# A gate that takes raw rows: centred weights, and 1 / std applied to the gate's result

## The chip, the cores and the metric

The kernel runs on one core of a Trainium2 chip. The metric is device time in microseconds, the median of several executions. The engines are TensorE (PE, its weight loads shown apart as PEld), VectorE (DVE), ScalarE (ACT), GpSimd (POOL) and SyncE (SP), which issues most DMAs. Each engine works through its own queue in order, and waits there for what an instruction needs from others.

## The reference

8192 tokens (2 sequences of 4096) of 512 channels:

```python
xn = _layernorm(x, axis=-1)                # (x - m) / sqrt(v + eps), no affine part
s = recurrence(xn, delta, alpha, beta, gamma, omega)   # causal convolution per channel, plus xn * omega
gate_logits = xn @ Wg.T + bg               # 8 experts
topk_vals, topk_idx = top_k(gate_logits, 2)
gate_w = softmax(topk_vals)
ffn = sum over the two experts of gate_w * (xn @ We[e].T + be[e])
out = x + s * silu(ffn)
```

All of it is float32.

## The kernel before

The work has three stages on one core, and their order on every engine is the order of the program: a helper (`InOrder`, lines 31 to 58) chains each instruction to the one before it on its engine, and all of them are recorded at its line 58.

Setup and first stage (lines 446 to 714). Tokens come in 64 chunks of 128, four chunks (`LC`) to a group, 16 groups (`NQ`). `load(q)` brings group q, 1 MB, into one of four buffers `xt_b` (`NX`). The recurrence's kernel is made first: VectorE, GpSimd and ScalarE make exponentials, GpSimd `coef_w`, and TensorE adds 256 small matmul instructions up in the PSUM tile `k_ps` (lines 547 to 557). `kernel_out` takes `k_ps` through VectorE and stores it to `k_dram`.

Then a loop over q runs these helpers:
- `stats_of(q)`: VectorE's mean and variance of four chunks, into `stats[:, c, 2:4]`. `stats_of(0)` stands right after the `k_ps` matmuls in the program.
- `root(q)`, on ScalarE, and `rest(q)`, on VectorE: `stats` then holds -mean / std and 1 / std.
- `apply(q, i, engine)`: one chunk is normalised from `xt_b` into `xn`, which lies in `big` as (channel, chunk), so that one chunk's channels lie 64 elements apart. Chunk 0 of a group is ScalarE's, the others are GpSimd's, a few VectorE's.
- `turn_chunk(q - 1, i)`: TensorE transposes four blocks of the chunk into a PSUM tile `pt`, and ScalarE copies that back into `xt_b`, over the rows of x.
- `gate(q - 1)`: 16 f32 matmuls (32 instructions) with `wg_sb` as the loaded weights and the transposed rows moving, into `lq`; VectorE copies it to `lqs`.
- `gate_end(q - 2)`: TensorE turns `lqs` back into `lt`; VectorE adds the bias and writes `logits`.
- `load(q + 3)`, on SyncE's queue, once `gate(q - 1)` has read the buffer.

Line 636 on is the loop itself, with its order. The `pt`, `lq`, `lt` tiles share six PSUM buffers (`ps_y`). After the loop the last group is transposed (line 697), the recurrence is begun (`states`, `scan`, `from_chunks`), and the last two groups' gates are done between (lines 709 to 714).

Second stage (lines 967 to 998): the recurrence over 64 groups of channels. Between its groups stand the routing steps, at group 2 `top2(0)`, which reads all logits. `double_toep` copies a group's matrix to the other half of the partitions, on ScalarE for even groups, on GpSimd for odd ones. Third stage (line 1003 on): two passes of experts over sorted tokens, with indirect gathers and scatters by GpSimd.

Of the kernel before, what the change touches and what calls it, by code (L numbers as in the profile page):

```python
# [8 lines left out]
FP = mybir.dt.float32  # L9
# [4 lines left out]
ALU = mybir.AluOpType  # L14
AX = mybir.AxisListType

P = 128
# [44 lines left out]
def tile_ssm_then_moe(  # L62
# [28 lines left out]
    C, _, D = x_rev.shape  # L91
    T = C * P
    NE = w_e.shape[0]
    KD = D // P
# [22 lines left out]
    ident = const.tile([P, P], FP)  # L117
# [4 lines left out]
    io = InOrder(tc)  # L122
# [9 lines left out]
    def bc(ap, *shape):  # L132
        return ap.to_broadcast(list(shape))
# [160 lines left out]
    with ExitStack() as ab:  # L294
        abc = ab.enter_context(tc.tile_pool(name="ab_const", bufs=1))

        xn = big[:, 0:4, :].rearrange("p i (d c) -> p (i d) c", c=C)
# [10 lines left out]
        stats = abc.tile([P, C, 4], FP)  # L308
        gate_b = abc.tile([P, NE], FP)
        flip = abc.tile([P, P], FP)  # L310
        logits = abc.tile([P, C, NE], FP)
# [8 lines left out]
        ps_y = ab.enter_context(tc.tile_pool(name="ps_y", bufs=NR + 2, space=PSUM))  # L320
# [26 lines left out]
        def double_toep(g):  # L347

            copy = io.scalar.copy if g % NS in TO_ACT else io.gpsimd.tensor_copy
            copy(toep_of(g, 1 - g % 2), toep_of(g, g % 2))  # L350
# [95 lines left out]
        with ExitStack() as ph0:  # L446
            su = ph0.enter_context(tc.tile_pool(name="setup", bufs=1))
            xtp = ph0.enter_context(tc.tile_pool(name="xnT", bufs=2))

            LC = 4  # L450
            NQ = C // LC
            NX = 4

            xt_b = [
                big[:, 4, i * LC * D : (i + 1) * LC * D].rearrange("p (c d) -> p c d", d=D)
                for i in range(NX)
            ]

            def load(q):
                io.sync.dma_start(  # L460
                    out=xt_b[q % NX], in_=x_rev[q * LC : (q + 1) * LC].rearrange("c p d -> p c d")
                )
# [3 lines left out]
            wg_sb = su.tile([P, KD, 32], FP)  # L466
            io.sync.dma_start(out=par, in_=params)
            load(0)
            io.gpsimd.memset(wg_sb, 0.0)
            io.sync.dma_start(out=om, in_=omega)  # L470
            io.sync.dma_start(out=wg_sb[:, :, 0:NE], in_=w_g)
            io.sync.dma_start(out=gate_b, in_=b_g.to_broadcast([P, NE]))
# [25 lines left out]
            q = su.tile([P, G], FP)  # L498
# [6 lines left out]
            def stats_of(q):  # L505
                st = xtp.tile([P, LC, 6], FP, tag="st")
                for i in range(LC):
                    io.vector.bn_stats(st[:, i, :], xt_b[q % NX][:, i, :])
                    io.vector.bn_aggr(stats[:, q * LC + i, 2:4], st[:, i, :])
# [38 lines left out]
            for n, (tl, bq) in enumerate(units):  # L548
                for a in range(2):
                    for i in range(IL):  # L550
                        for j in range(NR):
                            g = (tl * NR + j) * NB + 2 * bq + a
                            io.tensor.matmul(
                                k_ps[32 * j : 32 * j + 32, tl, i, :], coef_w[:, g, i, :],
                                ex_b[:, n, j, a, :], start=n == 0 and a == 0 and i == 0,
                                stop=n == len(units) - 1 and a == 1 and i == IL - 1,
                            )
            stats_of(0)
            io.scalar.activation(q_half, lnq, AF.Exp, scale=float(H))
            powers = {}  # L560
# [44 lines left out]
            def turn_chunk(q, i):  # L605
                pt = ps_y.tile([P, KD, P], FP, tag="py", name="pt")
                for k in range(KD):
                    io.tensor.transpose(
                        pt[:, k, :], xn[:, k * P : (k + 1) * P, q * LC + i], ident
                    )  # L610
                io.scalar.copy(xt_b[q % NX][:, i, :], pt.rearrange("p k t -> p (k t)"))

# [14 lines left out]
            def gate_end(q):  # L627
                lt = ps_y.tile([P, LC, 32], FP, tag="py", name="lt")
                io.tensor.transpose(lt.rearrange("p c j -> p (c j)"), lqs_of.pop(q), ident)
                io.vector.tensor_add(  # L630
                    logits[:, q * LC : (q + 1) * LC, :], lt[:, :, 0:NE],
                    bc(gate_b.unsqueeze(1), P, LC, NE),
                )

            toeps = {}
# [2 lines left out]
            for q in range(NQ):  # L638
# [7 lines left out]
                if q >= 1:  # L646
                    for i in range(LC):
                        turn_chunk(q - 1, i)
                if q >= 2:
                    gate_end(q - 2)  # L650
# [45 lines left out]
            for i in range(LC):  # L696
                turn_chunk(NQ - 1, i)
# [9 lines left out]
            toeps[TB - 1] = load_toep(TB - 1)  # L707
            double_toep(DOUBLED)
            gate_end(NQ - 2)
            gate(NQ - 1)  # L710
            from_chunks(0, 1, pys0, toeps.pop(1))
            toeps[TB] = load_toep(TB)
            double_toep(DOUBLED + 1)
            gate_end(NQ - 1)


        rt = ab.enter_context(tc.tile_pool(name="route", bufs=1))
# [407 lines left out]
```

## Time and profile before

| | us |
|---|---|
| median of 3 runs (lowest, highest) | 931.26 (927.09, 931.91) |
| profiled execution: time | 937.24 |
| profiled execution: span, first to last instruction | 935.5 |
| TensorE busy over the span (7035 matmul instructions) | 813.0 |
| VectorE busy | 608.4 |
| ScalarE busy | 379.2 |
| GpSimd busy | 511.9 |
| granted TensorE clock, mean | 0.942 |

The first stage takes about the first 98 us, the recurrence goes on to about 312 us, and the experts take the rest. Busy times are those of one profiled execution. A row of a timeline has the start and the length in us, the engine, the line, the operation, what it writes and reads, how often it came in that stretch, and in brackets the idle time of the engine ahead of it with what ended it.

### The profile page before, as it was taken

How to read it: one execution, taken by the hardware profiler on the slowest of the kernel's cores; microseconds unless marked ns; L12 is line 12 of the kernel's file. 1: busy time of each engine (PE TensorE's matmuls, PEld its weight loads, DVE VectorE, ACT ScalarE, POOL GpSimd, SP SyncE). 2: the span in 40 equal slices, each digit the busy share in tenths (PEclk: the TensorE clock that was granted, in tenths of full speed). 3: DMA queues.
4: the chain of work that ended last, by engine and by line, in shares of the span. 5: the costliest groups of instructions: out<-in, count | busy, mean ns of one | idle time of the engine just before them, and what ended most of it. 6: DMA issues, size and time to landing. Idle time of an engine off the chain costs nothing.

```text
span 935.5 us, 18673 instructions
## 1 busy us (share of the span) xinstructions
PE 813.0 (87%) x7035; PEld 479.3 (51%) x7038; DVE 608.4 (65%) x1147; ACT 379.2 (41%) x699; POOL 511.9 (55%) x513
## 2 busy tenths in 40 slices
PE   3989878886885799999999999995989797899876
PEld 3767657776765454444444444442434343444432
DVE  7877676768783656666666663264768575576675
ACT  7777646766762322222222121232434333244242
POOL 6767204431444355555555556576767675767732
PEclk9999968998997799999999999998999898989978
DMA  4656115768899875555555566577676766866740
GB/s 157 224 212 183 25 30 28 179 143 212 230 220 336 241 261 203 182 187 190 202 201 183 203 206 237 185 261 245 202 241 207 243 206 199 251 197 214 251 146 28
DMA packets 112822, 181.22 MB, mean 194 GB/s; under 512 B 18910, under 2 KB 68446, under 8 KB 112736
## 3 DMA queue, kind: packets, MB, share of 16 engines
q0 software_dynamic: 38128, 127.05, 40.8%
q1 hardware_dynamic: 74608, 52.99, 21.6%
q8 instruction: 58, 0.95, 0.4%
q14 instruction: 28, 0.23, 0.1%
HBM read 112.50 MB, written 73.01 MB: 198 GB/s over the span
## 4 chain that ended last, share of the span: by engine, by line
PE 39%; issue 16%; DVE 14%; POOL 13%; ACT 8%; DMA 6%; another core or an unknown queue 4%; POOLq 0%; SPq 0%; DVEq 0%; ACTq 0%
PE pe L58 26%; PE pt L58 5%; ACT big L58 5%; DVE big L58 4%; POOL big L58 4%; DVE came_b L58 4%; PE py L58 4%; POOL out L58 3%; DMA toep_b<-k_dram 2%; PE ph L58 2%; DMA big<-yx_dram,x_idx 2%; POOL sg L58 2%; POOL yx_dram L58 1%; POOL yx L58 1%
## 5 line engine op out<-in xcount | busy, mean ns | idle before, releaser
L58 PE MATMUL pe<-big,xnT 128*128 x672 | 311.7, 608 | 0.0
L58 PE MATMUL pe<-big 128*128 x464 | 214.6, 607 | 0.7 <-DMA s_dram<-big 0.7
L58 PEld LDWEIGHTS pe<-big,xnT 128*128 128x128 f32 x672 | 125.0, 196 | 127.2 <-issue 127.2
L58 PEld LDWEIGHTS pe<-big 128*128 128x128 f32 x464 | 86.0, 195 | 89.2 <-issue 88.9
L58 ACT COPY xnT<-pt 128x512 f32<-128x512 f32 x84 | 48.9, 582 | 202.8 <-PE pt L58 123.5
L58 POOL DMA_INDIRECT out<-big,o_idx x71 | 78.6, 1107 | 71.5 <-DVE big L58 53.6
L58 ACT COPY big<-pt 128x512 f32<-128x512 f32 x122 | 68.8, 597 | 116.7 <-PE pt L58 90.4
L58 PEld LDWEIGHTS pt<-ident,big 128*128 128x128 f32 x544 | 75.5, 198 | 69.8 <-issue 38.1
L58 PE MATMUL pt<-ident,big 128*128 128x128 f32 x544 | 87.5, 299 | 27.1 <-ACT xnT L58 13.5
L58 ACT ACTIVATE big<-big 128x512 f32<-128x512 f32 x103 | 65.8, 649 | 110.9 <-DVE big L58 69.9
L58 PE MATMUL py<-big,toep_b 64*64 64x64 f32 x2048 | 89.1, 243 | 15.9 <-issue 6.6
L58 PEld LDWEIGHTS py<-big,toep_b 64*64 64x64 f32 x2048 | 78.2, 153 | 27.3 <-issue 12.3
L58 POOL DMA_INDIRECT yx_dram<-big,o_idx x47 | 47.8, 1017 | 74.2 <-DVE big L58 72.4
L58 POOL TENSOR_TENSOR val<-hot,token 128x568 bf16<-128x568 bf16 x32 | 39.2, 1226 | 81.1 <-DVE hot L58 42.9
L58 PEld LDWEIGHTS pt<-ident,xn 128*128 128x128 f32 x280 | 35.4, 145 | 63.1 <-issue 43.0
L58 POOL TENSOR_SCALAR big<-big,stats 128x512 f32<-128x512 f32 x44 | 55.8, 1348 | 21.1 <-ACT stats L58 11.3
L58 PE MATMUL pt<-ident,xn 128*128 128x128 f32 x280 | 44.1, 282 | 24.7 <-ACT xnT L58 14.9
L58 POOL DMA_INDIRECT big<-in_x,x_idx x52 | 51.4, 988 | 23.0 <-issue 16.0
L58 DVE TENSOR_TENSOR big<-pe,big 128x512 f32<-128x512 f32 x47 | 32.5, 692 | 48.1 <-PE pe L58 38.2
L58 POOL DMA_INDIRECT sg<-s_dram,x_idx x42 | 48.0, 1142 | 13.1 <-issue 11.0
L58 POOL COPY toep_b<-toep_b 64x512 f32<-64x512 f32 x32 | 23.6, 743 | 53.8 <-DMA toep_b<-k_dram 52.4
L58 DVE TENSOR_TENSOR big<-big 128x512 f32<-128x512 f32 x73 | 50.3, 689 | 3.4 <-issue 1.2
(154 smaller groups left out, 1158.4 us busy)
## 6 DMA issues: line engine op xcount, KB each, us to landing
big<-in_x_rev SPq DMA_DIRECT2D x16, 1024.0 KB
s_dram<-big SPq DMA_DIRECT2D x64, 256.0 KB
toep_b<-k_dram SPq DMA_DIRECT2D x64, 128.0 KB
big<-in_w_e SPq DMA_DIRECT2D x16, 512.0 KB
big<-in_b_e SPq DMA_DIRECT2D x8, 256.0 KB
out<-big,o_idx POOLq DMA_INDIRECT x71
big<-in_x,x_idx POOLq DMA_INDIRECT x52
yx_dram<-big,o_idx POOLq DMA_INDIRECT x47
```

Of the source, the lines that this page charges most:

```text
L58: return lambda *args, **kwargs: self.order.follow(make(*args, **kwargs))
```

## The change

The transposes, and with them the gate, take the rows of x as loaded. Layer norm's mean is taken out through the weights: each expert's column of `wg_sb` is centred over the 512 channels once, with a mean from four matmuls by a matrix of 1 / 512 (`mean_w`, filled by GpSimd in the setup) and a subtraction on VectorE ahead of `stats_of(0)`. 1 / std multiplies each group's gate result in `gate_end`, and the bias is added once to all logits, on GpSimd, after the last group.

```diff
             io.gpsimd.memset(wg_sb, 0.0)
+            mean_w = su.tile([P, P], FP)
+            io.gpsimd.memset(mean_w, 1.0 / D)
             io.sync.dma_start(out=om, in_=omega)
...
+            wm = ps_y.tile([P, 32], FP, tag="py", name="wm")
+            for k in range(KD):
+                io.tensor.matmul(wm, mean_w, wg_sb[:, k, :], start=k == 0, stop=k == KD - 1)
+            io.vector.tensor_sub(wg_sb, wg_sb, bc(wm.unsqueeze(1), P, KD, 32))
             stats_of(0)
...
                     io.tensor.transpose(
-                        pt[:, k, :], xn[:, k * P : (k + 1) * P, q * LC + i], ident
+                        pt[:, k, :], xt_b[q % NX][:, i, k * P : (k + 1) * P], ident
                     )
...
-                io.vector.tensor_add(
-                    logits[:, q * LC : (q + 1) * LC, :], lt[:, :, 0:NE],
-                    bc(gate_b.unsqueeze(1), P, LC, NE),
+                cs = slice(q * LC, (q + 1) * LC)
+                io.vector.tensor_tensor(
+                    logits[:, cs, :], lt[:, :, 0:NE],
+                    bc(stats[:, cs, 3].unsqueeze(2), P, LC, NE), ALU.mult,
                 )
...
             gate_end(NQ - 1)
+            io.gpsimd.tensor_tensor(logits, logits, bc(gate_b.unsqueeze(1), P, C, NE), ALU.add)
```

The normalised rows are still made, by the same passes, since the recurrence needs them.

## The prediction

> **What bounds the kernel now.** I read the stage busy times first: up to about 98 us the first stage (norm, transposes, gate) runs, to 312 us the recurrence, then the experts. The change touches the first stage and the gate's end, so I opened the timeline of the first 60 us, all engines together. In it, "big<-big,stats" is a normalising pass, "big<-pt" a copy of transposed rows, and root, rest, gate are the functions of those names.
>
> ```profile
> 10.71 6.49 PE L58 MATMUL k_ps<-big 128*32 128x64 f32 x256 [10.71 <-ACT big L58]
> 11.13 0.68 DVE L58 BATCH_NORM_STATS2 st<-big 128x6 f32<-128x512 f32 x1
> ...
> 14.23 0.18 DVE L58 BATCH_NORM_AGGREGATE stats<-st 128x2 f32<-128x6 f32 x1
> ...
> 16.05 0.30 ACT L58 ACTIVATE stats<-stats,eps 128x4 f32<-128x4 f32 x1
> 16.39 0.18 DVE L58 RECIPROCAL stats<-stats 128x4 f32<-128x4 f32 x1 [1.98 <-ACT stats L58]
> ...
> 17.37 1.53 ACT L58 ACTIVATE big<-big,stats 128x512 f32<-128x512 f32 x1 [1.02 <-DVE st L58]
> ...
> 20.76 0.39 DVE L58 COPY came_b<-k_ps 128x256 f32<-128x256 f32 x1
> ...
> 23.03 2.11 ACT L58 COPY big<-pt 128x512 f32<-128x512 f32 x4
> ```
>
> To be seen: VectorE finishes the statistics of chunk group 0 at 14.41, under the k_ps matmuls that keep TensorE until 17.20. It then idles 1.98 us for ScalarE's square root (16.05), so rest(0) is early at 16.39; from there to 21.65 VectorE runs without a gap (statistics of group 1, one normalise, k_ps out, rest(1)). ScalarE's first copies come at 23.03, behind its second normalise.
>
> In the loop, one of its slower turns:
>
> ```profile
> 26.30 0.29 DVE L58 COPY lqs<-lq 128x128 f32<-128x128 f32 x1 [0.53 <-PE lq L58]
> ...
> 27.30 0.70 DVE L58 BATCH_NORM_STATS2 st<-big 128x6 f32<-128x512 f32 x1 [0.71 <-DMA big<-in_x_rev]
> ...
> 30.64 0.30 ACT L58 ACTIVATE stats<-stats,eps 128x4 f32<-128x4 f32 x1 [1.16 <-DVE stats L58]
> ...
> 31.39 1.54 ACT L58 ACTIVATE big<-big,stats 128x512 f32<-128x512 f32 x1 [0.45 <-DVE stats L58]
> ...
> 32.68 2.13 ACT L58 COPY big<-pt 128x512 f32<-128x512 f32 x4
> ...
> 33.41 2.51 PE L58 MATMUL lq<-big,wg_sb 128*32 128x128 f32 x32 [0.17 <-ACT big L58]
> ```
>
> Gate(0) ends at 26.26, frees lqs and its buffer's next load; statistics (3.3), root and rest (0.75), normalise on ScalarE (1.3), four copies (2.13), last 26 gate matmuls (1.06), and gate(2) ends at 35.92: 9.66 us for two turns. A second circle runs through the four x buffers: a load takes some 5.4 us (issued 21.86, waited for until 27.30), and 5.4 + 8.5 us of the same steps is about 14 for three turns. Fifteen turns from 20.99 to 96.08 make 5.0 us each. TensorE looks full, but its weight loads wait 15.9 us in total for ScalarE's copies, and the transposes are in neither circle, except where the copies keep pace with them (four copies in 2.35 instead of 2.13 us in the faster turns).
>
> **Start: the new wait.** VectorE's subtraction of the column means stands ahead of stats_of(0) in its queue and needs wm, whose matmuls stand behind all 256 k_ps matmuls. Queued behind it: all statistics, root and rest of group 0, group 1, and kernel_out, behind whose k_dram store SyncE's queue holds load(3). wm is four f32 matmuls, each two instructions (the expert groups have eight per four): 8 weight loads of 128x128. Nearest row: contiguous transposes, one per 0.11 us (below), so 0.9 us, and 0.2 to 0.3 for the last to come out; by the 0.19 us duration of an expert's weight load 1.5. From the k_ps end (about 17.0 for the last start): 18.1, at most 18.8. Subtraction, 128x128 with a PSUM operand: lqs copies cost 0.29, so 18.4. Statistics 11.13 to 14.41 are 3.28: 21.7. Root and latency 0.34: rest(0) at 22.1 instead of 16.39. From rest(0) on VectorE had no gap before, so all that follows moves: **+5.7 us** (5.2 with weight loads at half the nearest price, 6.3 with the dear one). The square root's table load is over by 16.05 and not waited for.
>
> **Loop: shorter transposes.** Before, 16 strided transposes; contiguous ones stand in the expert stage, here the weight-load timeline of both:
>
> ```profile
> 26.19 2.42 PEld L58 LDWEIGHTS pt<-ident,big 128*128 128x128 f32 x16 [0.20 <-issue]
> ```
>
> ```profile
> 403.40 0.36 PEld L58 LDWEIGHTS pt<-ident,xn 128*128 128x128 f32 x3 [0.29 <-issue]
> ```
>
> Sixteen starts (to the next load at 28.50) in 2.31 are 0.144 each; three in 0.36, the last lasting 0.14, are 0.11. So some 0.6 us per turn. The Trainium skill, "TensorE: Matmul & The Clock Gate", section LDWEIGHTS, prices a weight load by its columns alone, which would save nothing; the rows differ by stride at equal columns (median 258 against 140 ns), and I take the rows. By the page the tail gain below is zero and the sum 0.65 higher. Within the loop the 0.6 us becomes waiting for copies: those still stand behind ScalarE's normalise, which waits for rest. That the transposes need no normalised rows frees nothing else, since their copies overwrite x and must wait for the normalising passes to have read it. In the loop I take **-0.2**, one load (63.27, which waited 1.16 us) issued earlier; ends 0 and -1.
>
> After the last turn TensorE runs without a gap from the 16 transposes on to the matmuls that release VectorE's scan at 106.74 (the chain of waits):
>
> ```profile
> 96.15 2.55 PE pt L58 x16
> 98.70 1.49 PE ph L58 x64
> ```
>
> Here the saving counts once: **-0.65** (0 to -0.9).
>
> **A cold TensorE at the loop's start.** Freed transposes of group 0 run right behind wm and are done by about 20.2; then TensorE waits until copies(0), 23.03 + 5.7 = 28.7. The windows of 3.41 us in which the clock steps show what such a gap does (columns: length; busy us of PE, PEld, DVE, ACT, POOL; granted clock):
>
> ```profile
> 46.47:49.89 3.42, 2.04 (x15) 1.80 (x13) 2.49 (x8) 3.42 (x8) 2.41 (x3) 1.00 0.81 304
> 49.89:53.30 3.41, 3.07 (x38) 2.07 (x39) 1.11 (x4) 2.96 (x6) 0.75 (x1) 1.00 0.02 5
> ...
> 111.33:114.74 3.41, 1.15 (x22) 0.87 (x22) 3.13 (x7) 3.36 (x7) 0.61 (x1) 0.97 0.17 38
> 114.74:118.15 3.41, 3.28 (x88) 2.77 (x92) 3.27 (x5) 1.59 (x3) 0.00 (x0) 0.50 0.15 38
> ```
>
> A window with 1.15 us of PE halves the clock of the next; the new gap of 8.5 us holds a whole empty one. So gate(0) and transposes(1) start cold. Cold rates: four pw transposes take 1.11 instead of 0.65 us, 32 py matmuls 1.97 instead of 1.18, so 1.7 times. Gate(0)'s last 26: +0.75 us. Transposes(1), 3.0 us instead of 1.8, then pace the copies: gate(1) ends 1.3 to 2 us late. Gate(0)'s 0.75 partly hides under load(3)'s 0.71 us; gate(1)'s delay passes through lqs to the statistics of group 4. I take **+1.2**, ends 0.4 and 3. TensorE is then filled for over 6.8 us, so at least one full window, and warms: the window 128.39 to 131.81, busy throughout, ended a cold stretch. Against that stands the same page, section PE-mode transpose: transposes do not count as busy for the clock. Then the loop stays cold, at some 1.7 us per turn. The first row above speaks against it: that window holds nothing but transposes, and the next is still at 1.00. I take the row; the rule is a rival.
>
> **Rest.** The gate's multiply replaces an add of the same 128x32 shape (0.17 us): nothing. The mean_w memset (0.20 by the wg_sb row) lies in POOL's 0.81 us wait for lnq. The bias add, 128x512 on POOL: 1.34 by the "big<-steps,lnq" row; it waits for the last gate_end (104.76), ends about 106.2, while top2 takes logits at 110.75: hidden by the scan and 4.5 us to spare; without that cover 1.4. POOL's toep copy for group 5 is queued behind it and moves from about 96 to 107; group 5 is multiplied at 122.14. All free.
>
> **Sum:** 5.7 + 1.2 - 0.2 - 0.65 = +6.05. The recurrence and the experts start from the gate's results and the loop's end, and their loads are issued from the same order, so the shift arrives at the end. The profiled execution, 937.24 (935.5 span and what lies around it), becomes 943.3; it was 6.0 above the median of the runs, so the median 931.26 becomes **937.3**.
>
> **Rivals.** (1) The loop is TensorE's after all: 16 x 0.63 = 10.1 us saved, so 5.7 + 1.2 - 10.1 = -3.2, 928.1: not slower. For it: PE is busy over 3.0 of 3.41 us in most windows there. Against: 15.9 us of waits for ScalarE. It decides from 0.46 us reaching the circle per turn (6.9 / 15). (2) The cold loop: 14 x 1.7 = +24, 961. (3) The shift arrives in part: the clock's windows run on their own time, one cold window costs or saves about 1.7 us, and some eight cold stretches lie before 312 us; where two or three fall better, about 933.
>
> **How the numbers follow.** Forecast 0.60, own range 932.5 to 941.5; rival (1) 0.12, (2) 0.08, (3) 0.20. Half a per cent (4.7 us) is about what a measurement tells from no change: 935.9 and 926.6. Slower: 0.85 of the forecast, all of (2), a fifth of (3): 0.63. Faster: a third of (1) and traces of the others: 0.06. Same: 0.31. The range 931 to 946 leaves out most of (1) and all of (2).
>
> **What would show it.** Reciprocal of group 0 near 22 us; a PE gap of 8 us and clock 0.50 there; load(3) issued near 27.5; turns again about 5.0 us; the first scan about 6 us late; POOL's add ending before top2. Wrong if turns shrink to 4.6 us, if the clock stays low beyond about 40 us, or if wm finishes before 17 us.

## The result

Median of 18 runs 935.87 us (927.87 to 944.06), the kernel before beside it 930.17 (923.88 to 939.22): ratio 1.0075, 95% interval 1.005 to 1.010, so 4.7 to 9.3 us slower. The ratio compares fast runs alone and is not the quotient of the two medians, which is 1.0061. The forecast was 937.3 against 931.26, 6.05 us slower.

The changed kernel's timeline from 9 to 62 us, all engines, the rows that answer to those shown of before:

```profile
10.61 6.51 PE L58 MATMUL k_ps<-big 128*32 128x64 f32 x256 [10.61 <-ACT big L58]
17.04 1.08 PE L58 MATMUL wm<-wg_sb,mean_w 128*128 128x32 f32 x8
17.96 1.94 PE L58 MATMUL pt<-ident,big 128*128 128x128 f32 x16
18.16 0.29 DVE L58 TENSOR_TENSOR wg_sb<-wg_sb,wm 128x128 f32<-128x128 f32 x1 [7.06 <-PE wm L58]
...
22.02 0.18 DVE L58 RECIPROCAL stats<-stats 128x4 f32<-128x4 f32 x1 [0.37 <-ACT stats L58]
...
27.30 32.72 SPq L58 DMA_DIRECT2D big<-in_x_rev  x7
...
28.45 2.13 ACT L58 COPY big<-pt 128x512 f32<-128x512 f32 x4
...
29.18 3.37 PE L58 MATMUL lq<-big,wg_sb 128*32 128x128 f32 x32 [9.27 <-ACT big L58]
...
32.58 0.29 DVE L58 COPY lqs<-lq 128x128 f32<-128x128 f32 x1 [1.39 <-PE lq L58]
```

VectorE waits 7.06 us for wm, which TensorE makes behind k_ps. The reciprocal of group 0 comes at 22.02 instead of 16.39, load(3) at 27.30 instead of 21.86, the first copies at 28.45 instead of 23.03, and TensorE stands for 9.27 us ahead of gate(0). From lqs(0), the first copy of a gate's result, to the last group's transposes the loop then takes 69.37 us (32.58 to 101.95), before it took 69.78 (26.30 to 96.08).

The chain of waits behind the loop (start, length, what), first of before, then of the changed kernel:

```profile
106.74 1.28 DVE came_b L58 x2
...
108.11 2.71 DVE came_b L58 x2
```

```profile
102.02 1.90 PE pt L58 x16
103.91 1.49 PE ph L58 x64
...
111.95 1.28 DVE came_b L58 x2
...
113.33 2.34 DVE came_b L58 x2
```

The transposes start 5.87 us later than before (102.02 against 96.15) and VectorE's product behind the ph matmuls 5.21 later. The experts' first product starts 6.49 us later, at 319.13 instead of 312.64. The span of this one execution is nevertheless 934.5, shorter than the 935.5 of before. The gap closes in the experts' second pass: VectorE's first sum there (`big<-pe,big`) starts 6.5 us later than before (609.8 against 603.3), its last 0.6 us earlier (925.8 against 926.4). The change touches nothing in that pass, so single executions differ there by more than the change is worth, and the comparison rests on the runs together.

### The profile page after: what moved, and what is told of

It is laid out like the page before. It is cut to its first block, busy times and chain, and to the rows that moved or that the text cites. A ratio compares the mean times of both kernels' runs of the same rounds, so it can differ in the third digit from the quotient of the medians.

```text
span 934.5 us, 18653 instructions
## 1 busy us (share of the span) xinstructions
PE 803.9 (86%) x7046; PEld 469.0 (50%) x7046; DVE 609.9 (65%) x1148; ACT 377.4 (40%) x699; POOL 511.7 (55%) x515
## 4 chain that ended last, share of the span: by engine, by line
PE 49%; issue 13%; DVE 10%; POOL 10%; ACT 7%; DMA 6%; another core or an unknown queue 4%; POOLq 0%; DVEq 0%; SPq 0%; ACTq 0%
PE pe L58 31%; PE pt L58 7%; ACT big L58 5%; PE py L58 5%; DVE big L58 4%; POOL big L58 3%; DVE came_b L58 3%; PE ph L58 2%; PE lq L58 2%; DMA big<-yx_dram,x_idx 2%; POOL out L58 2%; DMA toep_b<-k_dram 1%; POOL yx_dram L58 1%; POOL yx L58 1%
## 5 line engine op out<-in xcount | busy, mean ns | idle before, releaser
L58 PE MATMUL pe<-big 128*128 x464 | 210.8, 598 | 0.6 <-DMA s_dram<-big 0.6
L58 PEld LDWEIGHTS pt<-ident,big 128*128 128x128 f32 x544 | 65.2, 144 | 58.0 <-issue 43.9
L58 PE MATMUL pt<-ident,big 128*128 128x128 f32 x544 | 77.3, 281 | 16.1 <-ACT big L58 11.6
L58 PE MATMUL lq<-big,wg_sb 128*32 128x128 f32 x512 | 36.4, 294 | 17.8 <-ACT big L58 14.8
```

What stands on the lines that cost most here:

```text
L58: return lambda *args, **kwargs: self.order.follow(make(*args, **kwargs))
```

## The experiments

They ran on other chips, where the kernel before takes 896 to 897 us; each ratio is to runs of the kernel before on the same chip. Each timeline is of one execution. The theory is that of the prediction: the statistics wait for wm behind k_ps. Rival A puts the loss on TensorE's halved clock after its gap, rival B on the multiply and the late bias.

**The wait without its cause, and the wait alone**

`wm_first` moves three lines:

```diff
+            wm = ps_y.tile([P, 32], FP, tag="py", name="wm")
+            for k in range(KD):
+                io.tensor.matmul(wm, mean_w, wg_sb[:, k, :], start=k == 0, stop=k == KD - 1)
             k_ps = ps_r.tile([P, KT, IL, H], FP, tag="rt", name="k_ps")
...
-            wm = ps_y.tile([P, 32], FP, tag="py", name="wm")
-            for k in range(KD):
-                io.tensor.matmul(wm, mean_w, wg_sb[:, k, :], start=k == 0, stop=k == KD - 1)
             io.vector.tensor_sub(wg_sb, wg_sb, bc(wm.unsqueeze(1), P, KD, 32))
```

> The changed kernel with the four wm matmuls ahead of the k_ps matmuls in TensorE's order, nothing else moved. Theory (VectorE's statistics wait for wm behind k_ps): the subtraction runs at about 11 us without a wait, the reciprocal of group 0 is back at about 16.4 us, the scan's release comes near 106.1 us (before 106.74, changed 111.95), and the time is 0.999 to 1.000 of the kernel before. Rival A (the cost is TensorE's cold clock after its gap): a gap of 4 us is left between transposes(0) and gate(0), so a good part of the loss stays, 1.003 or more. Rival B (the multiply and the late bias cost): 1.006 as in the change.

Measured: 894.21 against 896.75 us, ratio 0.9986 (0.9964 to 1.0008). The same kernel a second time, on another chip:

> wm_first once more, on the same chip as own_turned: the theory's 0.998 to 1.000, and the profile against which the turns of own_turned are read.

896.32 against 896.67, ratio 0.9984 (0.9960 to 1.0009). VectorE's timeline of `wm_first`, then TensorE's row of gate(0), and one microsecond of it (columns: length; busy us of PE, PEld, DVE, ACT, POOL; granted clock):

```profile
11.09 0.27 DVE L58 TENSOR_TENSOR wg_sb<-wg_sb,wm 128x128 f32<-128x128 f32 x1
16.34 0.18 DVE L58 RECIPROCAL stats<-stats 128x4 f32<-128x4 f32 x1 [1.78 <-ACT stats L58]
```

```profile
23.51 3.36 PE L58 MATMUL lq<-big,wg_sb 128*32 128x128 f32 x32 [4.91 <-ACT big L58]
```

```profile
22.00:23.00 1.00, 0.00 (x0) 0.00 (x0) 0.93 (x5) 1.00 (x2) 1.00 (x2) 0.50 1.09 281
```

The subtraction waits for nothing and the reciprocal is back at 16.34. TensorE's gap ahead of gate(0) is still 4.91 us, the clock is halved from about 21 to 28 us, and gate(0) takes 3.36 us, as long as in the change (3.37). Yet no loss can be measured: that is against rival A, and as multiply and late bias are in this kernel, against rival B. The release of VectorE's product (its start behind the ph matmuls, in the expectations the scan's release) was forecast for 106.1: the first profile has 108.56, the second 106.32, on loops that took 71.7 and 69.4 us. The longer one holds a wait of VectorE of up to 2.6 us for one load, the shorter none above 0.8; such a late load also stands in the profiles of `wait_only` (3.4 us), `sub_later` (4.1), `strided` (3.4) and `eight_adds` (3.3), and puts their releases late. What delays it was not looked for.

`wait_only` is the reverse: the kernel before, with wm and a subtraction that nobody reads.

```diff
+            mean_w = su.tile([P, P], FP)
+            io.gpsimd.memset(mean_w, 1.0 / D)
...
+            wm = ps_y.tile([P, 32], FP, tag="py", name="wm")
+            for k in range(KD):
+                io.tensor.matmul(wm, mean_w, wg_sb[:, k, :], start=k == 0, stop=k == KD - 1)
+            wg_c = su.tile([P, KD, 32], FP)
+            io.vector.tensor_sub(wg_c, wg_sb, bc(wm.unsqueeze(1), P, KD, 32))
             stats_of(0)
```

> The kernel before with mean_w, the four wm matmuls and the subtraction added where the change has them, the result going to a tile that nobody reads; transposes, gate and bias as before. Theory: the reciprocal of group 0 comes at 22.0 us, the scan's release near 112.4 us, ratio 1.006 to 1.007. Rival A (cold clock): transposes(0) still wait for the normalised rows and no long gap opens ahead of gate(0), so little is lost, 1.000 to 1.002. Rival B: nothing of the gate changes, 1.000.

901.27 us, ratio 1.0050 (1.0026 to 1.0074), a little under the 1.006 to 1.007 expected, which the interval holds. VectorE's timeline:

```profile
18.17 0.29 DVE L58 TENSOR_TENSOR wg_c<-wg_sb,wm 128x128 f32<-128x128 f32 x1 [7.03 <-PE wm L58]
22.03 0.18 DVE L58 RECIPROCAL stats<-stats 128x4 f32<-128x4 f32 x1 [0.37 <-ACT stats L58]
```

The interval also touches the change's, so that no rest for rival B is shown. One of its expectations was a miss: TensorE does get a gap here, 6.05 us ahead of the transposes, and a halved clock from about 21 to 31 us. So this run alone doesn't part theory and rival A; with `wm_first`, which has the clock and not the wait, it does. The release came at 115.94 instead of 112.4, behind the late load just named.

`sub_later` leaves wm where the change has it and lets VectorE make the first statistics ahead of the subtraction.

```diff
-            io.vector.tensor_sub(wg_sb, wg_sb, bc(wm.unsqueeze(1), P, KD, 32))
             stats_of(0)
+            io.vector.tensor_sub(wg_sb, wg_sb, bc(wm.unsqueeze(1), P, KD, 32))
```

> The changed kernel with the subtraction one place later on VectorE, after the statistics of group 0. Theory: these run at 11 to 14.4 us, VectorE then waits for wm until 18.2, the reciprocal of group 0 comes at 18.5 us (2.1 after the kernel before), the scan's release near 108.2 us, ratio 1.001 to 1.002. Rival A: the gap of TensorE ahead of gate(0) shrinks from 9 to some 6 us and still holds a whole window, so the loss stays at 1.005 or more. Rival B: 1.006.

898.38 us, ratio 1.0014 (0.9989 to 1.0038). The reciprocal comes at 18.75 us, 2.4 after that of before (k_ps itself ended 0.4 later here). The release was forecast for 108.2 and came at 112.39, again behind a late load. TensorE's clock is halved from about 24 to 31 us, and the interval still excludes rival A's 1.005. Over `wm_first` (16.34), `sub_later` (18.75) and the change (22.31 in `change_again` below) the ratio rises with the reciprocal: 0.9986, 1.0014, 1.0077. The intervals of neighbours meet; those of the first and the last do not.

**The cold clock**

`kept_warm` and `kept_warm_long` are the change with identity transposes in the gap, 72 and 88 of them.

```diff
+                if q == 1:
+                    fill = ps_w.tile([P, P], FP, tag="hw", name="fill")
+                    for _ in range(NFILL):
+                        io.tensor.transpose(fill, ident, ident)
```

> The changed kernel with 72 extra transposes of the identity on TensorE between transposes(0) and gate(0), some 8 us of work in the gap, read by nobody. Theory: gate(0) ends about 0.85 us earlier than in the change, but the statistics of group 3 hardly start earlier; the scan's release stays within 0.5 us of 111.95, ratio 1.005 to 1.0075. Rival A (cold clock): most of the loss is gone, 1.002 or less. Rival B: as the change.

> The changed kernel as it is, for a profile on the same chip as the three runs beside it. Theory: reciprocal of group 0 at 22.0 us, ratio 1.005 to 1.008.

> As kept_warm, with 88 instead of 72 identity transposes, so that TensorE's filled stretch reaches to gate(0) at about 29 us; in kept_warm it ended at 27.7 and one window at half clock was left (30.2 to 33.6). Theory: gate(0) runs at full clock and ends 0.8 us earlier than in change_again, the end of the loop moves by less than 0.5 us, ratio within 0.002 of change_again. Rival A (the cold clock costs): ratio at least 0.003 below change_again. For the clock: if transposes count as work the windows from 20 to 29 us stay at 1.00; if not, the clock is halved by 27 us at the latest.

`kept_warm` took 904.10 us, ratio 1.0080 (1.0041 to 1.0120); its filling ended at 27.7, too early: the clock was halved from 30.6 to 34.0, and gate(0) still took 3.36 us. `change_again` took 901.37, ratio 1.0077 (1.0037 to 1.0117), and `kept_warm_long` 903.63, ratio 1.0093 (1.0061 to 1.0125). Stretches of 3.41 us, first of the change, then of `kept_warm_long`, in the columns as above:

```profile
16.60:20.01 3.41, 3.30 (x64) 2.97 (x52) 1.78 (x6) 0.00 (x0) 0.00 (x0) 1.00 0.02 5
20.01:23.43 3.42, 0.00 (x0) 0.00 (x0) 2.91 (x10) 1.13 (x2) 0.75 (x1) 0.92 0.00 0
23.43:26.84 3.41, 0.00 (x0) 0.00 (x0) 3.27 (x10) 0.99 (x2) 1.81 (x2) 0.50 0.00 0
...
30.25:33.67 3.42, 3.42 (x37) 2.59 (x37) 1.43 (x6) 2.22 (x4) 3.02 (x3) 0.58 0.54 202
33.67:37.08 3.41, 3.33 (x47) 2.48 (x46) 2.98 (x11) 2.32 (x6) 1.42 (x3) 1.00 0.85 311
```

```profile
20.39:23.80 3.41, 3.41 (x34) 3.41 (x33) 2.90 (x10) 1.17 (x2) 0.79 (x1) 1.00 0.00 0
23.80:27.21 3.41, 3.41 (x34) 3.41 (x33) 3.27 (x10) 1.02 (x2) 1.86 (x2) 1.00 0.02 5
```

The change's TensorE is at half clock from about 23 to 33 us, as forecast. In `kept_warm_long` two whole stretches hold nothing but transposes and the clock stays at 1.00, through to gate(0). So transposes kept the clock up here; the sentence of the Trainium skill that the prediction set aside ("TensorE: Matmul & The Clock Gate", section PE-mode transpose) does not fit these f32 transposes. Whether transposes alone bring a halved clock back, no run shows. No gain shows in the times: `kept_warm_long` lies 0.0016 above `change_again`, where rival A wanted it at least 0.003 below. But each interval is 0.003 to 0.004 wide to either side, so 1.2 us (0.0013) cannot be told from nothing by them. VectorE's timeline of `kept_warm_long` shows one place where the gain goes:

```profile
32.15 0.29 DVE L59 COPY lqs<-lq 128x128 f32<-128x128 f32 x1 [0.53 <-PE lq L59]
33.34 0.70 DVE L59 BATCH_NORM_STATS2 st<-big 128x6 f32<-128x512 f32 x1 [0.90 <-DMA big<-in_x_rev]
```

lqs(0) is 0.67 us earlier than in `change_again` (32.82), and the statistics of group 3 then wait 0.90 us for load(3): they start at 33.34, in `change_again` at 33.03. The end of the loop was forecast to move by less than 0.5 us; in this pair of profiles the last transposes start 1.1 us earlier than in `change_again` (102.08 against 103.20), which is within what loops of one kernel differ by (71.7 and 69.4 above).

**The transposes by themselves**

`strided` is `wm_first` with the normalised rows transposed, and ones in the multiply.

```diff
-                        pt[:, k, :], xt_b[q % NX][:, i, k * P : (k + 1) * P], ident
+                        pt[:, k, :], xn[:, k * P : (k + 1) * P, q * LC + i], ident
...
-                    bc(stats[:, cs, 3].unsqueeze(2), P, LC, NE), ALU.mult,
+                    bc(one_c[:, cs].unsqueeze(2), P, LC, NE), ALU.mult,
...
```

> wm_first with the transposes taking the normalised rows again, 64 elements apart, and the gate's result multiplied by ones. Theory: against wm_first the 16 transposes of a turn take 2.6 instead of 2.0 us, the turns keep their length, the scan's release comes 0.6 us later than it would, ratio 0.9990 to 1.0005 (wm_first 0.9986). Rival (the loop is TensorE's): 16 times 0.6, 9 us slower than wm_first, 1.008.

896.05 us, ratio 0.9991 (0.9968 to 1.0015), in the theory's range and not to be told from `wm_first`; the rival's 1.008, 9 us above `wm_first`, is excluded. The weight loads of the transposes (ns: lowest, median, highest), first of the change, then of `strided`:

```profile
L58 PEld LDWEIGHTS pt<-ident,big x256: 137/140/231, 17.8 to 103.5; 128*128 128x128 f32 x128
```

```profile
L58 PEld LDWEIGHTS pt<-ident,big x256: 219/258/270, 18.5 to 101.7; 128*128 128x128 f32 x128
```

That 256 loads of such different length make no measurable difference says that the loop's length is not TensorE's.

**The bias**

`eight_adds` puts seven adds of zeros ahead of the change's one.

```diff
-            io.gpsimd.tensor_tensor(logits, logits, bc(gate_b.unsqueeze(1), P, C, NE), ALU.add)
+            zero_b = su.tile([P, NE], FP)
+            io.gpsimd.memset(zero_b, 0.0)
+            for b in [zero_b] * 7 + [gate_b]:
+                io.gpsimd.tensor_tensor(logits, logits, bc(b.unsqueeze(1), P, C, NE), ALU.add)
```

> The changed kernel with eight bias adds on GpSimd in a row instead of one, seven of them of zeros. Theory: one add is hidden with 4.2 us to spare (it ends at 111.4 us, top2 reads logits at 115.6); seven more at 1.27 us are 8.9 us, so top2 comes 4.7 us later; VectorE's work behind it moves by that at most, ratio 1.008 to 1.013. Rival B (the bias add is already on the path): 8.9 us more, 1.017.

911.91 us, ratio 1.0149 (1.0097 to 1.0202): the interval holds most of the theory's range and rival B's 1.017 too, so the times do not decide; the timelines do. GpSimd's and VectorE's, of the longest of the six runs (922.07 us), whose loop ran some 4.6 us longer than the change's:

```profile
114.70 10.94 POOL L58 TENSOR_TENSOR logits<-logits,zero_b 128x512 f32<-128x512 f32 x7 [9.69 <-DVE logits L58]
125.72 1.27 POOL L58 TENSOR_TENSOR logits<-logits,gate_b 128x512 f32<-128x512 f32 x1
```

```profile
117.91 3.99 DVE L58 TENSOR_TENSOR_SCAN came_b<-decay,came_b 128x512 f32<-128x512 f32 x2
127.03 0.69 DVE L58 TENSOR_REDUCE top<-logits 128x64 f32<-128x512 f32 x1 [5.13 <-POOL logits L58]
```

top2 waits 5.13 us. Counted from the last group's multiply it comes 12.67 us later here (114.36 to 127.03), in the change 5.80 (109.78 to 115.58): seven adds delay it by 6.9 us, not by 4.7. The scans beside the adds take 3.99 instead of the change's 2.34 us and the adds 1.56 instead of 1.27, which was not expected. In the change itself the one add ends at 111.39 and top2 runs at 115.58 without a wait, and that is against rival B.

**The circles of the loop**

If TensorE isn't what holds the turns, opening the two circles that the prediction named should shorten them. `lqs_later_load3` is `wm_first` with lqs copied one turn later, behind the next statistics, gate_end moved behind root and rest, and load(3) issued ahead of the k_dram store.

```diff
                     stats_of(q + 1)
+                if q >= 2:
+                    gate_out(q - 2)
...
                 if q == 0:
+                    load(3)
                     kernel_out()
...
-                if q >= 2:
-                    gate_end(q - 2)
                 if q + 1 < NQ:
                     root(q + 1)
                     rest(q + 1)
+                if q >= 2:
+                    gate_end(q - 2)
...
```

`gate_out` is the copy of lq to lqs, taken out of `gate`.

> wm_first with two waits of the loop's circles moved: VectorE copies lqs of a gate one turn later, after the next statistics, so that these no longer wait for TensorE's gate; and load(3), which has a free buffer, is issued ahead of the k_dram store. Theory (circle gate, lqs, statistics, root, rest, normalise, copies, gate, 9.66 us per two turns): without the lqs link the turns are held by the loads' circle, 14 us per three turns, 4.7 us instead of 5.0, so 15 turns gain 3 to 5 us and the time is 0.993 to 0.996. Rival (the loads' circle alone sets the turns at 5.0): only load(3)'s 0.7 us, 0.998.

903.19 us, ratio 1.0108 (1.0059 to 1.0158): slower, where 0.993 to 0.996 was forecast. The waits of its loop (us in total, times, longest):

```profile
PEld lt L58 <- DVE lqs L58: 24.3, 13, 3.2
...
DVE st L58 <- DMA big<-in_x_rev: 11.1, 9, 2.0
```

The lt transpose stands ahead of the next gate in TensorE's order. In `wm_first` it waited for lqs once, 1.1 us; now its waits make 24.3 us. VectorE's waits for the gates fall from 7.9 to 0.8 us, and its waits for loads rise from 5.2 to 11.1. A gate that ends late lets its buffer's load start late, so the wait seems to have moved from VectorE to TensorE and back to VectorE; this chain is read from the waits and was not tested alone.

`own_turned` takes the link from gate to load away, on top of `wm_first`: transposed rows go to one buffer of their own (mean_w lies in `flip`, not used until later, to find the room), load(q + 3) is issued right after the transposes of group q - 1, no longer after gate(q - 1), and load(3) ahead of the k_dram store. `own_turned_lqs` adds the later lqs copy, with lt two turns later so that TensorE finds it done.

```diff
+            turned_b = [su.tile([P, LC, D], FP, name=f"turned{i}") for i in range(1)]
...
-                io.scalar.copy(xt_b[q % NX][:, i, :], pt.rearrange("p k t -> p (k t)"))
+                io.scalar.copy(turned_b[q % len(turned_b)][:, i, :], pt.rearrange("p k t -> p (k t)"))
...
+                if 0 < q < NQ - 3:
+                    load(q + 3)
...
```

In `own_turned_lqs` this follows:

```diff
+                if q >= 3:
+                    gate_end(q - 3)
                 if q >= 2:
-                    gate_end(q - 2)
+                    gate_out(q - 2)
...
```

> wm_first, and the transposed rows go to a buffer of their own instead of over x, so that a buffer of x is free once normalised and transposed; load(q + 3) is issued right after the transposes of group q - 1, load(3) ahead of the k_dram store. Theory: the loads' circle (gate, load, statistics, root, rest, normalise, copies, gate) loses its link from gate to load, VectorE's DMA waits in the loop (5.2 us in wm_first) go, and the turns fall from 4.8 to about 4.5 us by the lqs circle: 0.994 to 0.997. Rival (the lqs circle alone sets the turns): 0.998.

> own_turned with lqs copied one turn later, after the next statistics, and its transposes back two turns later, so that TensorE never waits for lqs ahead of a gate (in lqs_later_load3 that wait was 24.3 us). Theory: with both circles open the turns are held by VectorE's or ScalarE's own 4.3 us, 15 turns gain some 3 us over own_turned: 0.990 to 0.995. Rival (DMA carries no more than 1 MB in 5 us): no more than own_turned.

`own_turned`: 891.98 against 896.67 us, ratio 0.9959 (0.9940 to 0.9978). `own_turned_lqs`: 889.93, ratio 0.9933 (0.9911 to 0.9954). Both beat the kernel before and the change. The last group's transposes in `wm_first_again`, `own_turned` and `own_turned_lqs`, from TensorE's timelines:

```profile
96.32 1.97 PE L58 MATMUL pt<-ident,big 128*128 128x128 f32 x16
```

```profile
93.33 1.97 PE L58 MATMUL pt<-ident,big 128*128 128x128 f32 x16
```

```profile
91.77 1.97 PE L58 MATMUL pt<-ident,big 128*128 128x128 f32 x16
```

VectorE's waits for loads in the loop are 3.1 us in the first, none in the second and 1.0 in the third. So in these profiles opening the loads' circle brought some 3 us, the later lqs copy 1.6 more up to that point; how much of it is load(3)'s alone is not separated. The ratios are 0.9984, 0.9959 and 0.9933: only the first and the third lie clear of each other's intervals. The release of VectorE's product then comes at 103.33 and 103.58: in the third kernel TensorE waits 1.48 us ahead of the last gate, behind the loop. Why its median is lower all the same isn't shown.

## Why the prediction was right

- **Start, +5.7.** Right in mechanism and size: the reciprocal moved by 5.63 us. wm took 1.08 us for its 8 instructions where 0.9 and 0.2 to 0.3 were put down, the subtraction 0.29. `wm_first` takes the loss away, `wait_only` makes most of it alone: the cause is shown from both sides.
- **Copies within the loop, -0.2.** Not told apart. The loop as a whole is 0.4 us shorter between the two profiles, while two executions of `wm_first`, on two chips, differ by 2.3 us.
- **Tail, -0.65.** The shift falls from 5.87 to 5.21 us between the last transposes and the release of VectorE: 0.66. The price came from the row of contiguous transposes, not from the price by columns alone in the Trainium skill ("TensorE: Matmul & The Clock Gate", section LDWEIGHTS), under which nothing would be gained: 16 of them now take 1.97 us, before 2.62.
- **Cold TensorE, +1.2.** The step that failed is the delay's way on. Gap and halved clock came as forecast, and gate(0) ended 0.86 us later than the shift of its copies (5.42 us), 0.75 forecast. But the clock rose again at about 33 us, amid transposes(1): these took 2.27 us, not 3.0, and gate(1) ended only some 0.7 us later than that shift, not 1.3 to 2. Nor did the delay pass "through lqs to the statistics of group 4". VectorE copied lqs(1) without a wait in both kernels, first before, then the change:

```profile
31.27 0.28 DVE L58 COPY lqs<-lq 128x128 f32<-128x128 f32 x1
```

```profile
36.85 0.28 DVE L58 COPY lqs<-lq 128x128 f32<-128x128 f32 x1
```

The shift is 6.28 us at lqs(0), 5.58 at lqs(1) and 5.64 at lqs(2) (35.96 to 41.60): what gate(0) added was gone one turn later. So in this pair of profiles the term is 0; the medians could not tell 1.2 us from it. Its lower end, 0.4, was the better value. That one full stretch of work warms the clock came true here, but the kernel before has one, busy throughout, that did not:

```profile
138.63:142.05 3.42, 3.42 (x68) 3.04 (x62) 1.90 (x3) 0.00 (x0) 0.00 (x0) 0.50 0.00 0
142.05:145.46 3.41, 1.77 (x34) 1.69 (x31) 3.34 (x8) 2.90 (x6) 0.00 (x0) 0.50 0.21 52
```

- **The rest, free.** Multiply, memset and one add: right, as `wm_first` holds them all. The add ended 4.2 us ahead of top2, 4.5 forecast; `eight_adds` shows that the cover is finite. The moved toep copy was not quite free but a small gain: before, it ran beside the second pair of scans (copy 1.57 us, scans 2.71), now it is over by then (0.61 and 2.34), and at top2 the shift is 4.83 us (110.75 to 115.58).
- **Rivals.** (1), TensorE's loop, is excluded by `strided`. (2), the cold loop, didn't come; apart from the start the clock was halved once more in the loop, for 3.41 us from 57.0. (3), a shift that arrives in part, would have made some 2 us and lies below the 4.7 to 9.3 of the runs. The forecast sum without the cold term is 4.85, near the 5.21 and 4.83 of this pair of profiles. Why the experts' start shows 6.5 us in this pair is open.
- **The sum.** Its mechanism, the wait for wm, is shown. That 6.05 lies so near the middle of the measured interval is in part luck: it holds 1.2 us that did not last, and the runs cannot tell 4.85 from 6.05.

## What to carry to other kernels

A one-off preparation is priced by the queue in front of it: four matmuls and a subtraction of 1.4 us cost most of the 5 to 9 us, since they stood behind 256 matmuls on one engine and ahead of the first statistics on another; the same instructions ahead of k_ps cost nothing that could be measured. Before a shorter operation is counted as a gain, find the circles that set the turn: 0.6 us less TensorE work in each of 16 turns showed as 0.66 us once, behind the loop. When a link of a circle is opened, look for what stands behind the moved instruction in every queue, as the lt transpose did; with a buffer freed earlier, and lt moved back together with lqs, the same loop gained about 0.5 per cent (0.9984 to 0.9933).

## What the runs showed of the hardware

An f32 weight load of 128 columns depended on where they lie: a median of 140 ns for columns side by side, 258 at 64 elements apart, and 0.11 against 0.144 us from one transpose to the next. Two stretches of 3.41 us full of transposes kept TensorE's clock at 1.00, where the same time left empty halved it. GpSimd's f32 work and VectorE's scans slowed each other when they ran at the same time: in the kernel before, a copy took 1.57 instead of 0.61 us and a pair of scans 2.71 instead of 2.34; in `eight_adds` an add took 1.56 instead of 1.27 and the scans 3.99. And a single profile's span would have told the wrong sign here: 934.5 against 935.5 us, with medians 5.7 us apart the other way.
